# Layer 3's attention: scores computed once and kept in SBUF, instead of once by rows and once by columns

## The chip, the cores and the metric

The kernel runs on one core of a Trainium2 chip. Four compute engines work side by side, each through its own queue in order: TensorE (PE; its weight loads are PEld), VectorE (DVE), ScalarE (ACT) and GpSimd (POOL). SyncE (SP) issues transfers. TensorE writes only to PSUM, eight banks of 2 KB on each of 128 partitions; VectorE and ScalarE read it, GpSimd works in SBUF alone. The metric is the device time of one execution, in microseconds. All numbers are fp32.

## The reference, cut to what matters

Four layers follow one another on four batches of 512 rows of 512 channels: a cross attention (layer 0), two recurrent layers of the RWKV kind (1 and 2), and layer 3, a cross attention of perceiver form with an MLP. Only layer 3 is touched. Its inputs are the context (`x` below), the result of layer 2 (`latents`), and a key mask of the context:

```
h = concatenate([x, latents], axis=1)              # 1024 keys
q = (latents @ q_w + q_b)                          # 512 queries, 16 heads of 32
k, v = h @ kv_w + kv_b
attn = einsum('bkhd,bnhd->bhkn', q, k) / 32
attn = where(mask, attn, -inf)                     # 512 context keys may be masked
attn = softmax(attn)
out = einsum('bhkn,bnhd->bkhd', attn, v) @ out_w + out_b + latents
out = rmsnorm(out) * postnorm_w
return gelu(out @ mlp_w1 + mlp_b1) @ mlp_w2 + mlp_b2 + latents
```

The softmax needs the largest score of every query, over all 1024 keys, ahead of the exponentials.

## The kernel before

Layers 0 to 2 end at about 2402 us, layer 3 fills the rest. The engines' instructions stand in the order in which the program writes them; `layer3` is a generator whose first parts are run beside the tail of the recurrent layers (each `yield` ahead of `"closed"` gives the word back to `recurrent`), and the loop at the end of `layer3` writes the rest.

A unit is one batch and four heads (the four 32-row strips `r` of a 128-channel block `m`), so there are 16 units. In the loop, each unit has eight steps (`NB` = 8 blocks of 128 keys), and three units are in work at once:

- `least(u, lt, a)` (L1196) makes, for one block of 128 queries and one half of the keys, four scores of 128 queries by 512 keys (`psc`), queries on partitions. VectorE adds the key mask as a row (`nm`, or `zeros`) and takes the minimum of the negated scores into one column of `mx`, written by L1206.
- `spread` (L1217), once a unit, turns that column by TensorE transposes (`pb`) into rows that are alike on all partitions, and ScalarE copies them to `mb`.
- `turned(u, s)` (L1230), a unit later, makes the scores again, keys on partitions (`pst`: 128 keys by 512 queries for four heads); VectorE subtracts `mb` on the way out of PSUM (L1237).
- `weights` (L1239): ScalarE's exponential over 2048 elements, with the mask as a bias per partition for the context keys; GpSimd adds the blocks into `acc`, whose sum over partitions is the softmax's denominator.
- `values` (L1262), two steps later: the products with `v` add up in one PSUM bank, `po`.
- `counted`, `inverted`, `divided`: the denominator by a product of `acc` with ones, its reciprocal, and the product with `po` into `y`.

Between these stand two further generators that the loop takes piece by piece: `prep` (q, k and v of the next unit: five pieces, and two more for a new batch in `begin`), and `finish` (output product, residual, norm, transposes and the MLP of the batch before: 38 pieces of one to eight products). `piece(early)` or `piece(rest)` takes one per step, and `behind` decides whether a second one is taken. `finish` of the last batch comes after the loop. Matrix products of a whole array go through the helper `mm` (L73), so its line holds most of TensorE's work; there the tiles tell the groups apart: `ph` and `po<-l_m,hT` are the MLP, `pout` the output product, `pq`, `pk`, `pv` belong to `prep`. ScalarE changes its table of functions whenever an exponential follows a gelu or the other way round.

PSUM in the loop is one pool of seven banks for everything (`ps_s`) and one bank for `po`.

Of the kernel before, what the change touches and what calls it, by code (L numbers as in the profile page):

```python
# [8 lines left out]
F32 = mybir.dt.float32  # L9
# [21 lines left out]
def tile_xattn_rwkv_perceiver(ctx: ExitStack, tc: tile.TileContext, t: dict, out: bass.AP):  # L31
# [1070 lines left out]
    def layer3():  # L1102
# [3 lines left out]
        T2 = 2 * P  # L1106
        with ExitStack() as pools:
# [10 lines left out]
            nc.vector.tensor_scalar(cols[:, :, 0], cols[:, :, 0], -1.0 / HD, None, ALU.mult)  # L1118
# [3 lines left out]
            zeros = cp.tile([P, L], F32, name="zeros")  # L1122
            nc.gpsimd.memset(zeros, 0.0)
# [3 lines left out]
            b2 = row_bcast(cp, t["L3_b2"], C, "b2")  # L1127
            st = [{} for _ in range(B)]

            def begin(b):  # L1130
# [4 lines left out]
                mi = bp.tile([P, L], I32, tag="sc", name="mi", bufs=2)  # L1135
                nc.sync.dma_start(mi, t["mask3"][b : b + 1, :].to_broadcast([P, L]))
                nm = bp.tile([P, L], F32, tag="nm", name="nm", bufs=2)
                nc.vector.tensor_scalar(nm, mi, 0.0, 1e30, ALU.is_equal, ALU.mult)
                d["nm"] = nm, zeros
# [5 lines left out]
                for k in range(KC):  # L1145
                    pt = ps_s.tile([P, L], F32, tag="s", name="ptx")
                    for i in range(LT):
                        nc.tensor.transpose(pt[:, i * P : (i + 1) * P], xn[b][i][:, k * P : (k + 1) * P], ident)
                    nc.scalar.copy(xT[:, k, :], pt)
                    if k % 2:  # L1150
                        yield

            def prep(b, m):
# [7 lines left out]
                q = d["q", m] = bp.tile([P, L], F32, tag="q", name="q", bufs=3)  # L1161
                pm = ps_s.tile([P, L], F32, tag="s", name="pq")
                mm(pm, [(w3["q"][:, k, :], d["xT"][:, k, :]) for k in range(KC)])
                nc.scalar.activation(q, pm, AF.Identity, bias=cols[:, m, 0:1], scale=-1.0 / HD)
                yield
                kT = d["k", m] = bp.tile([P, 2, L], F32, tag="kT", name="kT", bufs=3)
                v = d["v", m] = bp.tile([P, NB, P], F32, tag="v", name="v", bufs=3)
                for a, src in enumerate((d["cT"], d["xT"])):
# [3 lines left out]
                    yield  # L1172
                    pm = ps_s.tile([P, LT, P], F32, tag="s", name="pv")
# [9 lines left out]

            def row_scores(lhsT, rhs, name):

                ps = []
                for r in range(NR):
                    rs = slice(32 * r, 32 * r + 32)  # L1190
                    psc = ps_s.tile([P, L], F32, tag="s", name=name)
                    nc.tensor.matmul(psc, lhsT[rs], rhs[rs], start=True, stop=True, tile_position=(32 * r, 0))  # L1192
                    ps.append(psc)
                return ps

            def least(u, lt, a):  # L1196

                b, m = u
                d = st[b]
                if (lt, a) == (0, 0):  # L1200
                    d["mx", m] = bp.tile([P, 2, LT, NR], F32, tag="mx", name="mx", bufs=2)
                mx = d["mx", m]
                ps = row_scores(d["q", m][:, lt * P : (lt + 1) * P], d["k", m][:, a, :], "psc")
                for r in range(NR):
                    sc = bp.tile([P, L], F32, tag="sc", name="sc", bufs=2)
                    nc.vector.tensor_tensor_reduce(  # L1206
                        sc,
                        ps[r],
                        d["nm"][a],
                        1.0,  # L1210
                        mx[:, 0, lt, r : r + 1] if a else 3.0e38,
                        ALU.add,
                        ALU.min,
                        mx[:, a, lt, r : r + 1],
                    )

            def spread(u):  # L1217

                b, m = u
                d = st[b]  # L1220
                mb = d["mb"] = bp.tile([P, NR, L], F32, tag="mb", name="mb", bufs=1)
                for r in range(NR):
                    pb = ps_s.tile([P, L], F32, tag="s", name="pb")
                    for lt in range(LT):
                        nc.tensor.transpose(  # L1225
                            pb[:, lt * P : (lt + 1) * P], d["mx", m][:, 1, lt, r : r + 1].to_broadcast([P, P]), ident
                        )
                    nc.scalar.copy(mb[:, r, :], pb)

            def turned(u, s):  # L1230

                b, m = u
                d = st[b]
                ps = row_scores(d["k", m][:, s // LT, s % LT * P : (s % LT + 1) * P], d["q", m], "pst")
                w = d["w", s] = sp.tile([P, NR, L], F32, tag="aT", name="aT", bufs=3)
                for r in range(NR):
                    nc.vector.tensor_tensor(w[:, r, :], ps[r], d["mb"][:, r, :], ALU.subtract)  # L1237

            def weights(u, s):  # L1239

                b, m = u
                d = st[b]
                w = d["w", s]
                wf = w.rearrange("p r l -> p (r l)")
                if s < LT:
                    nc.scalar.activation(wf, wf, AF.Exp, bias=d["mc"][:, s : s + 1], scale=-1.0)  # L1246
                else:
                    nc.scalar.activation(wf, wf, AF.Exp, scale=-1.0)  # L1248
                if s == 1:
                    acc = d["acc", m] = sp.tile([P, NR, L], F32, tag="acc", name="acc", bufs=1)  # L1250
                    nc.gpsimd.tensor_tensor(acc, d["w", 0], w, ALU.add)  # L1251
                elif s > 1:
                    nc.gpsimd.tensor_tensor(d["acc", m], d["acc", m], w, ALU.add)  # L1253

            def columns(po, lhsT, rhs, **kw):

                for r in range(NR):
                    nc.tensor.matmul(  # L1258
                        po[32 * r : 32 * r + 32, :], lhsT(r), rhs[:, r, :], tile_position=(0, 32 * r), **kw
                    )  # L1260

            def values(u, s):  # L1262

                b, m = u
                d = st[b]
                if s == 0:
                    d["po"] = ps_o.tile([P, L], F32, tag="o", name="po")
                v = d["v", m]
                columns(
                    d["po"], lambda r: v[:, s, 32 * r : 32 * r + 32], d["w", s], start=(s == 0), stop=(s == NB - 1)  # L1270
                )

            def counted(u):

                b, m = u
                d = st[b]
                pn = d["pn"] = ps_s.tile([P, L], F32, tag="s", name="pn")
                columns(pn, lambda r: ones, d["acc", m], start=True, stop=True)

            def inverted(u):  # L1280
                d = st[u[0]]
                rs = d["rs"] = bp.tile([P, L], F32, tag="sc", name="rs", bufs=2)
                nc.vector.reciprocal(rs, d["pn"])

            def divided(u):
                b, m = u
                d = st[b]
                if "y" not in d:
# [220 lines left out]
```

## Time and profile before

| | us |
|---|---|
| median of 3 runs | 3721.07 (3719.92 to 3722.31) |
| span of the profiled execution, first to last instruction | 3715.9 |
| layer 3 from the first score after the recurrent layers (2402.6) | 1313 |
| of it attention of the first batch, to the first `pout` (2642.0) | 239 |
| of it attention beside the finishing of batches 0 to 2 (to 3576.4) | 934 |
| of it the last finish | 140 |

The profiled execution is a run of its own, whose time is its span and what lies around it: 5.2 us less by its span than the median of the runs. The page gives busy time over the whole span; in a group's line stand line, engine, operation, tile out<-in, shapes and count, then busy time and the mean of one in ns, then the idle time ahead of it and what ended it. A window's line gives, for each engine, busy time and the number of instructions, then the granted TensorE clock as a share, DMA share and GB/s. A timeline's line is start, length, engine, line, operation, and in brackets the idle time before it.

### The profile page before, as it was taken

To read this page: it belongs to the slowest core of one execution; us is meant where nothing else is said; L and a number is where in the kernel's file an instruction comes from. 1 tells how busy PE (TensorE), PEld (TensorE's weight loads), DVE (VectorE), ACT (ScalarE), POOL (GpSimd) and SP (SyncE) were. 2 spreads that over 40 slices of the span, in tenths; PEclk is the share of its full clock that TensorE was granted. 3 is DMA by queue.
4 is the path that set the end of the run, shared out by engine and by line. 5 is a ranking of instruction groups with operands and counts; after the bars stand their busy time and mean duration, and the time that the engine had idled before them with its cause. 6 is when DMAs were issued, how large, how long until landed. Compare 5 with 4: busy or idle time off the path is not lost. (4 is left out here: it accounts for less than half of the span.)

```text
span 3715.9 us, 52436 instructions
## 1 busy us (share of the span) xinstructions
PE 3545.8 (95%) x20544; PEld 1885.9 (51%) x20544; DVE 2728.7 (73%) x4601; ACT 1675.7 (45%) x2550; POOL 1743.4 (47%) x850
## 2 busy tenths in 40 slices
PE   8999999998899999999999988999999999999989
PEld 3333333365566665666666644444455444544446
DVE  6777777679988888888888883388855676667531
ACT  4777676544444444444444433233344334434421
POOL 4777777524444444444444443065533343444430
PEclk9999999999999999999999998999999999999999
DMA  4000000056677777777777775300022212121223
GB/s 154 24 12 24 12 9 21 24 130 140 146 177 175 177 187 182 176 175 177 177 175 177 177 167 134 102 26 18 23 88 77 72 52 88 60 71 35 97 97 125
DMA packets 188806, 386.67 MB, mean 104 GB/s; under 512 B 18128, under 2 KB 44880, under 8 KB 186512
## 3 DMA queue, kind: packets, MB, share of 16 engines
q1 hardware_dynamic: 150256, 251.72, 21.2%
q0 software_dynamic: 38304, 131.61, 19.4%
q8 instruction: 162, 2.65, 0.3%
q14 instruction: 84, 0.69, 0.1%
HBM read 247.50 MB, written 4.19 MB: 68 GB/s over the span
## 5 line engine op out<-in xcount | busy, mean ns | idle before, releaser
L1253 POOL TENSOR_TENSOR acc<-acc,aT 128x2048 f32<-128x2048 f32 x96 | 436.2, 4544 | 336.2 <-ACT aT L1248 219.6
L292 POOL TENSOR_TENSOR aT<-aT,nmT 128x1536 f32<-128x1536 f32 x124 | 428.6, 3460 | 206.1 <-ACT aT L290 182.8
L254 DVE CUSTOM_DVE_ANT_0 sc<-psc,nm 128x512 f32<-128x512 f32 x512 | 353.8, 691 | 146.8 <-PE psc L242 89.1
L1237 DVE TENSOR_TENSOR aT<-pst,mb 128x512 f32<-128x512 f32 x512 | 317.5, 681 | 163.2 <-PE pst L1192 163.2
L871 DVE TENSOR_TENSOR ry<-kv,o_r 128x1024 f32<-128x1024 f32 x256 | 398.6, 1598 | 7.2 <-PE pm L73 0.5
L866 DVE TENSOR_TENSOR_SCAN kv<-W,kv 128x1032 f32<-128x1032 f32 x128 | 295.9, 2311 | 0.0
L584 POOL DMA_DIRECT2D kv<-A x127 | 111.4, 877 | 358.0 <-DVE kv L839 220.0
L290 ACT COPY aT<-pst 128x512 f32<-128x512 f32 x372 | 196.5, 594 | 177.2 <-PE pst L279 176.8
L298 ACT ACTIVATE aT<-aT 128x2048 f32<-128x2048 f32 x128 | 246.7, 1929 | 5.5 <-POOL aT L292 4.8
L73 PE MATMUL ph<-nT,l_m 128*128 128x256 f32 x1024 | 235.9, 385 | 0.0
L73 PE MATMUL po<-l_m,hT 128*128 128x512 f32 x512 | 233.1, 601 | 0.0
L73 PEld LDWEIGHTS ph<-nT,l_m 128*128 128x128 f32 x1024 | 191.8, 191 | 64.2 <-issue 24.8
L1206 DVE CUSTOM_DVE_ANT_0 sc<-psc,zeros,mx 128x512 f32<-128x512 f32 x256 | 176.6, 745 | 56.2 <-PE psc L1192 47.1
L279 PE MATMUL pst<-q,km 32*128 32x512 f32 x1024 | 206.3, 639 | 9.4 <-DVE mxs L254 5.8
L1248 ACT ACTIVATE aT<-aT 128x2048 f32<-128x2048 f32 x64 | 122.3, 1910 | 190.6 <-DVE aT L1237 185.7
L1246 ACT ACTIVATE aT<-aT,mc 128x2048 f32<-128x2048 f32 x64 | 128.1, 2002 | 162.6 <-DVE aT L1237 156.3
L1206 DVE CUSTOM_DVE_ANT_0 sc<-psc,nm 128x512 f32<-128x512 f32 x256 | 161.1, 684 | 52.2 <-PE psc L1192 52.2
L242 PE MATMUL psc<-km,q 32*128 32x512 f32 x1024 | 197.8, 650 | 0.8 <-ACT q L223 0.8
L885 PE MATMUL py<-ry,k 128*32 128x512 f32 x1024 | 161.9, 625 | 38.3 <-DVE ry L871 25.6
L1192 PE MATMUL pst<-q,kT 32*128 32x512 f32 x1024 | 183.1, 649 | 0.0
L1192 PE MATMUL psc<-kT,q 32*128 32x512 f32 x1024 | 171.0, 644 | 12.3 <-DVE aT L1237 11.5
L1251 POOL TENSOR_TENSOR acc<-aT 128x2048 f32<-128x2048 f32 x16 | 72.5, 4532 | 234.2 <-ACT aT L1246 234.2
(266 smaller groups left out, 6999.6 us busy)
## 6 DMA issues: line engine op xcount, KB each, us to landing
l_m<-in_L_W SPq DMA_DIRECT2D x64, 1024.0 KB, 5.1
kv<-A POOLq DMA_DIRECT2D x127, 516.0 KB, 6.1
L_wk<-in_L_Wk SPq DMA_DIRECT2D x16, 1024.0 KB, 8.0
L_wr<-in_L_Wr SPq DMA_DIRECT2D x16, 1024.0 KB, 7.2
L_wv<-in_L_Wv SPq DMA_DIRECT2D x16, 1024.0 KB, 5.8
L_wg<-in_L_Wg SPq DMA_DIRECT2D x16, 1024.0 KB, 7.6
L_wo<-in_L_Wo SPq DMA_DIRECT2D x64, 256.0 KB, 4.9
L_fk<-in_L_fWk SPq DMA_DIRECT2D x16, 1024.0 KB, 6.8
```

The source lines that it names most:

```text
L73: nc.tensor.matmul(ps, lhsT, rhs, start=(i == 0), stop=(i == len(pairs) - 1))
L242: nc.tensor.matmul(psc, d["q"][g][rs, lt * P : (lt + 1) * P], d["km"][rs, a, :], start=True, stop=True, tile_position=(32 * r, 0),)
L254: nc.vector.tensor_tensor_reduce(sc, ps[r], d["nm"][lt], 1.0, -3.0e38, ALU.add, ALU.max, mxs[:, a, lt, c : c + 1])
L279: nc.tensor.matmul(pst, d["km"][rs, a, s * P : (s + 1) * P], d["q2", a][rs, :], start=True, stop=True, tile_position=(32 * r, 0),)
L292: nc.gpsimd.tensor_tensor(w[:, n:, :], w[:, n:, :], nmT[:, None, :].to_broadcast([P, NR - n, L]), ALU.add)
L298: nc.scalar.activation(w, w, AF.Exp)
L866: nc.vector.tensor_tensor_scan(flat(kv), flat(W[g % 2]), flat(kv), 0.0, ALU.mult, ALU.add)
L871: nc.vector.tensor_tensor(y, kv[:, 4 * h : 4 * h + 4, None, :TP].to_broadcast([P, 4, 2, TP]), d["r"][:, i].rearrange("p (o m) -> p o m", o ...
L1192: nc.tensor.matmul(psc, lhsT[rs], rhs[rs], start=True, stop=True, tile_position=(32 * r, 0))
L1206: nc.vector.tensor_tensor_reduce(sc, ps[r], d["nm"][a], 1.0, mx[:, 0, lt, r : r + 1] if a else 3.0e38, ALU.add, ALU.min, mx[:, a, lt, r : ...
L1237: nc.vector.tensor_tensor(w[:, r, :], ps[r], d["mb"][:, r, :], ALU.subtract)
L1253: nc.gpsimd.tensor_tensor(d["acc", m], d["acc", m], w, ALU.add)
```

## The change

Each unit is split in two halves of 256 queries (`h`), so there are 32 half units; each has four steps (`NS` = 4), a step being two blocks of 128 keys (`e`) for four heads and 256 queries. Scores are made once, keys on partitions, in a PSUM tile `ps` of four banks, of which there is one buffer (`ps_w`). VectorE takes the maximum of that tile into a running maximum `run` in SBUF (`largest`; masked keys get their bias in the same operation), and ScalarE copies the tile, with the mask as its bias, into SBUF (`kept`; six buffers `w`). After four steps `gathered` turns `run` by eight transposes (`ptm`) and VectorE reduces them to the maximum of each query, `spread` turns it back as before. In the next four steps `lowered` subtracts it in place, SBUF from SBUF, the exponential follows, then `values` and the GpSimd additions (`added`). A one-element `tick` is set by VectorE in each step and copied by GpSimd ahead of its additions, so that these begin behind VectorE's maximum of that step. The loop takes `prep` in steps 0, 4 and 6 of a unit (two, two and three pieces) and `finish` in the other five (two each); `prep` of the second unit runs beside the recurrent tail, where unit 0's `least` ran. PSUM is four banks for `ps`, three for all else, and one for `po`.

Beside this: `out_b` is added to the residual by GpSimd in `begin` and taken off `b2`, the scaling by 1/rms goes from VectorE to ScalarE (`scaled`), the transposes for the MLP's second half come after its first half, and the mask's row form with its transfers is gone.

```diff
-                mi = bp.tile([P, L], I32, tag="sc", name="mi", bufs=2)
-                nc.sync.dma_start(mi, t["mask3"][b : b + 1, :].to_broadcast([P, L]))
...
+                for x in xn[b]:
+                    nc.gpsimd.tensor_tensor(x, x, ob, ALU.add)
...
+            def scores(i):
+                (b, m, h), j = place(i)
+                d = st[b]
+                ps = ps_w.tile([P, NR, 2, HQ], F32, tag="w", name="ps")
+                a, s = divmod(2 * j, LT)
+                for e in range(2):
+                    for r in range(NR):
+                        rs = slice(32 * r, 32 * r + 32)
+                        nc.tensor.matmul(
+                            ps[:, r, e, :],
+                            d["k", m][rs, a, (s + e) * P : (s + e + 1) * P],
+                            d["q", m][rs, h * HQ : (h + 1) * HQ],
...
+            def kept(i):
...
+                w = ws[i] = sp.tile([P, NR, 2, HQ], F32, tag="w", name="w", bufs=6)
+                if a:
+                    nc.scalar.copy(w.rearrange("p r e q -> p (r e q)"), ps.rearrange("p r e q -> p (r e q)"))
+                else:
+                    for e in range(2):
+                        nc.scalar.activation(
+                            w[:, :, e, :], ps[:, :, e, :], AF.Identity, bias=d["mc"][:, s + e : s + e + 1]
+                        )
+            def largest(i):
...
+                for e in range(2):
+                    mc = d["mc"][:, s + e : s + e + 1]
+                    if a:
+                        nc.vector.tensor_tensor(run, ps[:, :, e, :], run, ALU.max)
+                    elif j or e:
+                        nc.vector.scalar_tensor_tensor(run, ps[:, :, e, :], mc, run, ALU.add, ALU.max)
+                    else:
+                        nc.vector.tensor_scalar(run, ps[:, :, e, :], mc, None, ALU.add)
+            def gathered(u):
...
+                for c in range(2):
+                    pt = ps_s.tile([P, NR, P], F32, tag="s", name="ptm")
+                    for r in range(NR):
+                        nc.tensor.transpose(pt[:, r, :], d["run"][:, r, c * P : (c + 1) * P], ident)
+                    nc.vector.tensor_reduce(mx[:, c, :], pt, AX.X, ALU.max)
+            def lowered(i):
...
+                nc.vector.tensor_tensor(w, w, mb, ALU.subtract)
+            def weights(i):
+                w = ws[i].rearrange("p r e q -> p (r e q)")
+                nc.scalar.activation(w, w, AF.Exp)
+            def added(i):
...
+                if j == 0:
...
+                    nc.gpsimd.tensor_tensor(d["acc", m, h], w[:, :, 0, :], w[:, :, 1, :], ALU.add)
+                else:
+                    for e in range(2):
+                        nc.gpsimd.tensor_tensor(d["acc", m, h], d["acc", m, h], w[:, :, e, :], ALU.add)
...
+            LOW, VAL, CNT = NS, NS + 1, NS + 3
+            yield from chain(begin(0), prep(0, 0), prep(0, 1))
+            first.close()
+            yield "closed"
+            sp = opened("l3s", 2)
+            ps_s = opened("l3ps", 3, space=PSUM)
+            ps_w = opened("l3pw", 1, space=PSUM)
+            po = opened("l3po", 1, space=PSUM).tile([P, 2, HQ], F32, name="po")
...
+            for i in range(NU + CNT + 1):
...
+                if i >= NS and i % NS == 0 and i <= NU:
+                    gathered(units[i // NS - 1])
+                if 0 <= i - VAL < NU:
+                    values(i - VAL)
...
+                    counted(units[done // NS])
+                if i < NU:
+                    scores(i)
+                if i >= NS and i % NS == 0 and i <= NU:
+                    spread(units[i // NS - 1])
+                low = i - LOW
+                if 0 <= low < NU and low % NS:
+                    lowered(low)
+                    weights(low)
+                if i < NU:
+                    largest(i)
+                    kept(i)
+                if 0 <= low < NU and low % NS == 0:
+                    lowered(low)
+                    weights(low)
+                if 0 <= low < NU:
+                    tick = sp.tile([P, 1], F32, tag="tick", name="tick")
+                    nc.vector.memset(tick, 0.0)
+                    nc.gpsimd.tensor_copy(mark, tick)
+                if 0 <= i - VAL < NU:
+                    added(i - VAL)
...
+                if c in (0, 4, 6):
+                    taken(early, 3 if c == 6 else 2)
+                else:
+                    taken(rest, 2)
```

## Prediction

> **What bounds the kernel now.** I read the page first, for the share of each engine:
>
> ```profile
> PE 3545.8 (95%) x20544; PEld 1885.9 (51%) x20544; DVE 2728.7 (73%) x4601; ACT 1675.7 (45%) x2550; POOL 1743.4 (47%) x850
> ```
>
> That is a mean over four layers. The change touches layer 3 alone, so I took the windows by stage: the first batch's attention, three stretches in which attention runs beside the finishing of the batch before (first `pout` at 2642.0), and the last finish.
>
> ```profile
> core 0: us, PE busy (x) PEld busy (x) DVE busy (x) ACT busy (x) POOL busy (x), PEclk, DMA share, GB/s
> 2402.00:2622.00 220.00, 218.42 (x1224) 99.44 (x1225) 181.14 (x409) 80.58 (x64) 123.75 (x29) 1.00 0.09 27
> 2622.00:2941.00 319.00, 315.84 (x1620) 154.96 (x1619) 210.99 (x440) 125.66 (x124) 135.03 (x37) 0.99 0.20 66
> 3272.00:3576.00 304.00, 296.02 (x1462) 144.00 (x1460) 186.39 (x367) 120.37 (x120) 137.48 (x37) 0.98 0.22 74
> 3576.00:3716.00 140.00, 129.35 (x436) 82.48 (x432) 28.82 (x42) 17.61 (x41) 7.11 (x8) 0.96 0.31 105
> ```
>
> TensorE is busy through all of layer 3; VectorE reaches 82% in the first stretch, 61 to 66% later. The TensorE timeline shows how a block is made: whole matrix products fill the time between the scores.
>
> ```profile
> 2916.98 3.72 PE L73 MATMUL ph<-nT,l_m 128*128 128x256 f32 x16
> 2920.63 1.14 PE L1192 MATMUL pst<-q,kT 32*128 32x512 f32 x8
> 2921.70 1.06 PE L1258 MATMUL po<-aT,v 128*32 128x512 f32 x8
> 2922.70 1.14 PE L1192 MATMUL psc<-kT,q 32*128 32x512 f32 x8
> 2923.77 3.70 PE L73 MATMUL po<-l_m,hT 128*128 128x512 f32 x8
> ```
>
> Start to start, a group of four score matmuls costs 1.07, a group of values 1.0, a piece of finish or prep 3.63 to 3.77 us. The groups give the prices of the other engines:
>
> ```profile
> L1253 POOL TENSOR_TENSOR acc<-acc,aT 128x2048 f32<-128x2048 f32 x96 | 436.2, 4544 | 336.2 <-ACT aT L1248 219.6 <-ACT aT L1246 116.6
> L1248 ACT ACTIVATE aT<-aT 128x2048 f32<-128x2048 f32 x64 | 122.3, 1910 | 190.6 <-DVE aT L1237 185.7 <-POOL acc L1253 4.7
> L1228 ACT COPY mb<-pb 128x512 f32<-128x512 f32 x64 | 32.7, 604 | 0.6 <-PE pb L1225 0.6
> L833 DVE TENSOR_TENSOR kv<-vr,o_k 128x1024 f32<-128x1024 f32 x128 | 155.5, 1215 | 25.2 <-ACT S L857 25.1
> L946 DVE TENSOR_TENSOR y<-y,bc 128x1024 f32<-128x1024 f32 x16 | 19.6, 1224 | 18.9 <-ACT bc L944 18.9
> ```
>
> Last, two timelines that decide the new step. VectorE's sum of two SBUF operands (normally 0.69) takes 1.63 because GpSimd's add, from 2671.30 to 2676.02, is in the way; and after 3.16 us of idle TensorE's next groups run at half pace (six score instructions in 3.27, where eight take 1.14).
>
> ```profile
> 2671.30 4.72 POOL L1253 TENSOR_TENSOR acc<-acc,aT 128x2048 f32<-128x2048 f32 x1
> ...
> 2674.94 1.63 DVE L1304 TENSOR_TENSOR ao<-ao,x 128x512 f32<-128x512 f32 x1
> ...
> 2680.36 3.27 PE L1192 MATMUL psc<-kT,q 32*128 32x512 f32 x6 [3.16 <-DVE aT L1237]
> ```
>
> **The new step.** There are 32 half units (four heads, 256 queries) of four steps, 128 steps in all. On TensorE a step is 1.1 of scores (two groups of 256 columns; twice the 0.44 that L689's 256-column groups take, plus the 0.2 by which 1.07 exceeds two such) and 1.0 of values. `psc`, 8.6 us a unit, goes. Each half unit adds eight transposes for the maximum, 0.95 by `pb`'s 1.84 for sixteen; the eight `pb` stay, and `pn` is 0.55. So a unit asks TensorE for 16.8 + 3.8 + 1.1 = 21.7 instead of 28.1 us (psc 8.6, pst 8.6, po 8.0, pn 1.0, pb 1.84): 6.4 less.
>
> VectorE, per step: subtract 2048 elements, 2.29 (1.224 for 1024 and 0.691 for 512 give the slope); maximum, two of 1024 from PSUM, 2.4. Per half unit: two reductions 1.4, reciprocal 1.7 (half of L1283's 3.35), product 0.4, the four ticks 0.4. ScalarE, per step: the exponential 1.91 and the new copy out of PSUM, 2.2 with the mask (0.687 for 512 plus 0.427, twice), 1.9 without. GpSimd: adds of 1024 cost 2.35 (between 1.27 for 512 and 4.53 for 2048), seven a half unit.
>
> **The new waits.** The score tile takes four banks and has one buffer. In the built program the copy waits for VectorE's maximum, and the next scores wait for the copy. So where nothing else is to be done a step costs scores 1.1, maximum 2.4, copy 2.2 and three hand-overs of some 0.07: 5.9 us. The subtraction has both operands in SBUF, and so do GpSimd's adds: 4.7 + 2.29 = 7.0 if each excludes the other. The row above shows VectorE held; the reverse shows in the same add: L1253 takes 4.72 where its median is 4.53, each time that a 1.5 us VectorE operation at L1309 ends inside it. I take 7.0; the other end is 5.9. At a half unit's border the chain is longer: from the end of the last maximum, transposes 1.0, values 1.0, scores 1.1, maximum 2.4, subtraction 2.3 to 3.4 (behind an add), exponential 1.9, then that block's values 1.0, the next scores 1.1, their maximum 2.4: about 15.5 for two steps, with hand-overs. Two more steps at some 5.6 to 7.0, one of them with the division, bring a half unit without pieces to 28.5. TensorE idles over 3 us twice in it and then runs at half pace; by the 3.27 us row that costs some 2 us. 30.5 a half unit, 61 a unit; ends 25.5 (VectorE's own 23.3 and one border gap of 2.2) and 34 (each border and every third step at half pace).
>
> The Trainium skill, SBUF — State Buffer, section Who interferes with whom, speaks against this subtraction: a VectorE instruction with two SBUF inputs contends with a GpSimd instruction that reads SBUF, and the one issued second is blocked until the first ends. By that rule the step without pieces is 7.0 and the first batch as summed below; were the lock one-sided it would be 5.9, and the first batch some 30 us shorter. The trace agrees for the side that it shows (1.63 instead of 0.69).
>
> **The sum by stages**, against the profiled execution: span 3715.9, median of the runs 3721.1, so 5.2 lie around it.
>
> 1. Up to the last recurrent product, 2402.6 now. Unit 0's eight `psc` groups leave that tail: 9.9 us on the chain of waits. Four new adds of `ob` (1.27 each) stand on GpSimd before `gn_rs` (L935), which the chain passes: +5. 2397.6.
> 2. To the first finish: step 38. Steps 0 to 3 have no subtraction, 5.9 each, and a first half unit of 27 with no GpSimd backlog: 48. Then 30 steps at 61 per eight: 229. Sum 277, against 2402.6 to 2642.0, 239: **+38**. prep's five pieces a unit lie in the border gaps.
> 3. Steps 38 to 134, beside finishes 0 to 2, two pieces of 3.65 a step: TensorE 9.4, VectorE under 8.2, ScalarE 8.6 (with two table loads of 1.28 and two to four gelus of 0.47), GpSimd 4.7. TensorE's content: scores 90 x 1.1, values 95 x 1.0, 23 borders x 1.9, 25 `pn` x 0.55 (together 252), ten preps x 18.8 and a piece (192), two begins x 4, three finishes x 135 (ph 235.9, po 233.1, pout 59.5, ptn 12.3, by four): 857. Gaps: step 6 of a unit has one piece, 0.5 x 12; two steps without a piece, 5.5 each; unit 15 has no prep to do, 25; the end of the last half unit 16; nT before its first product 9; gelus inside a pair of pieces 9: 76. 933, against 2642.0 to 3576.4, 934: **-1**. The 77 us that `psc` saves in twelve units go into these gaps and into the finishing pieces that now find less time to hide in. Ends of the gaps: 20 (most are covered) and 120.
> 4. Last finish: 139.5 now; the second half's transposes no longer stand ahead of the first product (4.1 us of idle) but the division comes before it, 2.5: 138.5.
>
> 2397.6 + 277 + 933 + 138.5 = 3746; plus 5.2: **3751 us**, 0.8% slower.
>
> Moved at no cost: scaling by 1/rms goes from VectorE (23.7 us in all) to ScalarE, hidden while a step has pieces; `ob`'s add leaves VectorE (11 us) for GpSimd, which has 20 of each 50 us busy. The row mask and its DMAs go; they lay beside other work. Table loads stay at 73.
>
> **Rivals.** (a) The gaps of stage 3 close: steps with two pieces leave VectorE and ScalarE time to be ahead, and TensorE's 95% busy row speaks for it. With 20 instead of 76 the time is 3695; it decides, against the loss of stage 2, from gaps under 38 us on: faster. (b) No measurable difference: stage 2 at its one-sided 5.9 a step, 30 less: 3721. (c) ScalarE becomes the bound in stage 3: its 8.6 stand only 0.8 under TensorE's 9.4, and the copy sits in its queue behind an exponential that waits for VectorE, with all gelus behind it. At 10.5 a step, 97 steps give 1018: 3836. Against it: 120 to 130 us busy in 304 to 331 now. That the work is not removed is excluded: the built order has no `psc` any more.
>
> **Numbers.** Forecast (3729 to 3800) 0.56, (a) 0.26, (b) 0.10, (c) and worse 0.08. Faster 0.26, same 0.10, slower 0.64; 0.2%, 7.4 us, is about what a measurement of this kernel can tell from no change. The range: stage 2 by 25.5 to 34 a half unit is -40 to +26, stage 3 by 20 to 120 is -56 to +44, stage 1 ±5. All together would be 3650 to 3826; 8 in 10 is 3695 to 3800. Within the forecast alone 3729 to 3790.
>
> **What would show it.** Right: in the first batch TensorE under 75% busy, a lower granted clock there, some 60 us between every second `pb`; subtractions far above 2.3 us on average; in the middle some 75 to 79 us a unit with TensorE still above 90%. Wrong: subtractions at 2.3 and units of 52 in the first batch (one-sided or no lock); middle units of 71 (rival a); ScalarE above 90% with TensorE waiting for the copy in the middle (rival c). The number falls first with the gaps of stage 3, which no row of before shows.

## The result and the profile after

The changed kernel takes 3804.1 us (median of 4 runs, 3798.5 to 3805.7), the kernel before 3720.6 on the same chip: ratio 1.0221, 95% interval 1.0206 to 1.0235. That is 83 us slower where 30 were forecast, and 4 us beyond the upper end of the range. The span of the profiled execution is 3802.2.

The windows of the changed kernel, cut at its first score (2398.1), at the first `pout` of each of the four finishes, and at its end; columns as before:

```profile
core 0: us, PE busy (x) PEld busy (x) DVE busy (x) ACT busy (x) POOL busy (x), PEclk, DMA share, GB/s
2398.00:2731.00 333.00, 220.01 (x1778) 130.59 (x1778) 217.22 (x193) 163.18 (x128) 192.70 (x99) 0.76 0.06 18
2731.00:3054.00 323.00, 297.85 (x2011) 184.55 (x2013) 207.18 (x202) 191.12 (x180) 171.85 (x101) 0.96 0.22 72
3054.00:3376.00 322.00, 296.65 (x2024) 183.99 (x2020) 208.19 (x202) 191.14 (x180) 172.67 (x101) 0.97 0.22 73
3376.00:3669.00 293.00, 252.79 (x1645) 153.29 (x1638) 175.48 (x173) 165.09 (x154) 161.17 (x91) 0.94 0.20 66
3669.00:3802.00 133.00, 127.80 (x432) 81.03 (x430) 19.54 (x34) 20.13 (x45) 7.13 (x8) 0.99 0.34 115
```

| stage | before | forecast | after |
|---|---|---|---|
| first score at | 2402.6 | 2397.6 | 2398.1 |
| first batch, to the first `pout` | 239 | 277 | 332.6 |
| beside finishes 0 to 2 | 934 | 933 | 938.0 |
| last finish | 139.5 | 138.5 | 133.6 |

By the span, the profiled execution lies 56 us above the forecast's 3746, and all of that is in the first batch (55.6; the other stages nearly cancel). There TensorE is 66% busy, at a granted clock of 0.76. No engine is full: VectorE has 65%, GpSimd 58%, ScalarE 49%. So it is waits, and the lower clock, that set this stage. TensorE's list of waits, first for this stage, then for the middle (us in all, times, longest):

```profile
PE ps L1199 <- ACT w L1220: 32.5, 8, 10.9
PE ptm L1249 <- DVE tick L1450: 22.3, 8, 3.4
PE po L1293 <- DVE y L1323: 22.3, 7, 4.8
PE po L1293 <- ACT w L1276: 19.4, 8, 5.5
PE ps L1199 <- ACT w L1217: 7.5, 3, 4.6
...
PE po L1293 <- ACT w L1276: 28.9, 18, 7.2
PE po L73 <- ACT hT L1374: 18.8, 12, 2.9
PE ph L73 <- DVE nT L1357: 16.3, 3, 5.5
PE po L1293 <- DVE y L1323: 13.8, 9, 5.1
PE ptx L1145 <- ACT xT L1146: 9.9, 2, 4.9
```

Scores waiting for the copy and transposes waiting for the maximum were in the forecast; values waiting for the division (`y`) were not. (The two halves of a unit have their sums in the one bank of `po`; in `bank`, below, where each has a bank of its own, this wait is gone.) The timeline of TensorE over most of a half unit shows what the waits do to the pace:

```profile
2507.38 1.15 PE L1199 MATMUL ps<-q,kT 32*128 32x256 f32 x16
2512.48 1.93 PE L1293 MATMUL po<-w,v 128*32 128x256 f32 x16 [3.95 <-ACT w L1276]
2514.19 1.08 PE L1293 MATMUL pn<-acc,ones 128*32 128x256 f32 x8
2515.29 1.21 PE L1199 MATMUL ps<-q,kT 32*128 32x256 f32 x16
2516.43 3.84 PE L73 MATMUL pv<-w3v,xT 128*128 128x128 f32 x32
2521.34 1.07 PE L1293 MATMUL po<-w,v 128*32 128x256 f32 x16 [1.07 <-DVE y L1323]
2522.34 1.15 PE L1199 MATMUL ps<-q,kT 32*128 32x256 f32 x16
2526.44 1.97 PE L1249 MATMUL ptm<-ident,run 128*128 128x128 f32 x8 [2.95 <-DVE tick L1450]
2528.34 1.94 PE L1293 MATMUL po<-w,v 128*32 128x256 f32 x16
```

After a gap of 3 to 4 us a group of values takes 1.93 instead of 1.07, eight transposes 1.97 instead of 1.04; after 1.07 us of gap the pace is kept. And this is the start of the stage, which has no subtraction yet:

```profile
2398.07 1.14 PE L1199 MATMUL ps<-q,kT 32*128 32x256 f32 x16
2398.25 0.69 DVE L1035 SCALAR_TENSOR_TENSOR xr<-xr,pv 128x512 f32<-128x512 f32 x1 [2.76 <-PE pv L73]
2399.23 0.86 POOL L584 DMA_DIRECT2D x<-xr  x1 [2.59 <-DVE xr L1035]
2405.18 1.28 DVE L1240 TENSOR_SCALAR run<-ps,mc 128x1024 f32<-128x1024 f32 x1 [6.25 <-DMA x<-xr]
2406.50 1.28 DVE L1238 SCALAR_TENSOR_TENSOR run<-ps,mc,run 128x1024 f32<-128x1024 f32 x1
2407.95 2.12 ACT L1220 ACTIVATE w<-ps,mc 128x1024 f32<-128x1024 f32 x2 [16.04 <-DVE run L1238]
2410.12 2.09 PE L1199 MATMUL ps<-q,kT 32*128 32x256 f32 x16 [10.90 <-ACT w L1220]
```

The maximum of the first tile waits 6.25 us for the transfer that carries the last rows out of the recurrent layers (`x<-xr`). The likely reason is in the program: the pool of `run` is opened when the recurrent layers' pools have been closed, so it can lie on memory that this transfer still reads. No run tested that. TensorE idles for 10.9 us, and the next scores run at half pace (2.09).

Taken apart by steps, the 55.6 us between the forecast's 277 and 332.6 are three:

- The start: scores of step 8 stand at 2463.7, 65.6 after the first; 48 was forecast. +17.6.
- Steps 8 to 38: 257.9 (scores of step 38 at 2721.6); 229 was forecast. +28.9.
- The end of the stage was counted one step early: step 38 takes pieces of `prep`, and the first `pout` (2730.6) is taken in step 39. +9.0.

### The profile page after: what moved, and what is told of

It reads as the page before. It is cut to its first block, busy times and chain, and to the rows that moved or that the text cites. A ratio compares the mean times of both kernels' runs of the same rounds, so it can differ in the third digit from the quotient of the medians.

```text
span 3802.2 us, 54498 instructions
## 1 busy us (share of the span) xinstructions
PE 3443.3 (91%) x21952; PEld 1972.7 (52%) x21952; DVE 2711.7 (71%) x3637; ACT 1930.9 (51%) x2758; POOL 1915.7 (50%) x1106
## 5 line engine op out<-in xcount | busy, mean ns | idle before, releaser
L1288 POOL TENSOR_TENSOR acc<-acc,w 128x1024 f32<-128x1024 f32 x192 | 491.5, 2560 | 7.8 <-POOL mark L1451 0.2
L254 DVE CUSTOM_DVE_ANT_0 sc<-psc,nm 128x512 f32<-128x512 f32 x512 | 354.1, 692 | 148.0 <-PE psc L242 90.3
L1451 POOL COPY mark<-tick 128x1 f32<-128x1 f32 x128 | 92.7, 724 | 556.9 <-DVE tick L1450 378.1
L1276 ACT ACTIVATE w<-w 128x2048 f32<-128x2048 f32 x128 | 244.5, 1911 | 200.4 <-DVE w L1272 187.7
L1272 DVE TENSOR_TENSOR w<-w,mb 128x2048 f32<-128x2048 f32 x128 | 321.5, 2522 | 1.8 <-ACT mb L1265 1.8
L298 ACT ACTIVATE aT<-aT 128x2048 f32<-128x2048 f32 x128 | 246.8, 1929 | 5.6 <-POOL aT L292 4.9
L1293 PE MATMUL po<-w,v 128*32 128x256 f32 x2048 | 160.1, 437 | 84.4 <-ACT w L1276 48.3
L1236 DVE TENSOR_TENSOR run<-ps,run 128x1024 f32<-128x1024 f32 x128 | 156.5, 1223 | 77.4 <-PE ps L1199 75.2
L1199 PE MATMUL ps<-q,kT 32*128 32x256 f32 x2048 | 170.1, 453 | 40.2 <-ACT w L1220 32.5
L1220 ACT ACTIVATE w<-ps,mc 128x1024 f32<-128x1024 f32 x128 | 135.6, 1110 | 118.0 <-DVE tick L1450 62.0
```

Of the source, the lines that this page charges most:

```text
L254: nc.vector.tensor_tensor_reduce(sc, ps[r], d["nm"][lt], 1.0, -3.0e38, ALU.add, ALU.max, mxs[:, a, lt, c : c + 1])
L298: nc.scalar.activation(w, w, AF.Exp)
L1199: nc.tensor.matmul(ps[:, r, e, :], d["k", m][rs, a, (s + e) * P : (s + e + 1) * P], d["q", m][rs, h * HQ : (h + 1) * HQ], start=True, stop ...
L1236: nc.vector.tensor_tensor(run, ps[:, :, e, :], run, ALU.max)
L1272: nc.vector.tensor_tensor(w, w, mb, ALU.subtract)
L1276: nc.scalar.activation(w, w, AF.Exp)
```

## Experiments

Theory A (chain): scores, maximum, copy, next scores, through the one PSUM tile, set a step. Theory B (exclusion): GpSimd's additions and VectorE's subtraction shut each other out, and that sets a step, as the prediction took it. Theory C (pace): TensorE's half pace after gaps lies on the path. Theory D: values wait for the division. Differences below are against the changed kernel's 3804.1; the kernel before took 3720.6 to 3723.5 beside these runs, so a difference of some 3 us between two runs says little. Stages are those of the profiled executions. In the cuts of the edits, `...` stands for lines left out.

**The additions taken away** (`no_adds`).

```diff
-                if j == 0:
+                if j == NS - 1:
                     d["acc", m, h] = sp.tile(...)
                     nc.gpsimd.tensor_tensor(d["acc", m, h], w[:, :, 0, :], w[:, :, 1, :], ALU.add)
-                else:
-                    for e in range(2):
-                        nc.gpsimd.tensor_tensor(d["acc", m, h], d["acc", m, h], w[:, :, e, :], ALU.add)
```

> Left out: GpSimd's additions of the denominator, all but the one of the last step of a half unit (one instruction of 2.36 us in place of seven), so the denominator is the sum of a quarter of the terms. Theory B (exclusion: a step of the first batch lasts 7 us or more because GpSimd's adds, 4.7, and VectorE's subtraction, 2.29, both with their operands in SBUF, shut each other out): subtractions come down from 2.52 to 2.3 us on average, the first stage (first score group to first pout, 332.6 us now) loses 1.1 us in each of some 34 steps, 35 to 45 us, total some 3762. Theory A (chain: scores, maximum, copy, scores through the one PSUM score tile set the step, and the subtraction fits into VectorE's wait for the next scores even when it is held): first stage -10 at most, total 3792 or more. Theory C (TensorE's half pace) says nothing of it: no change of the clock, 0.76.

Measured: 3785.9, -18.2; the first stage 326.1 (-6.5), the middle 925.6 (-12.4). The group of subtractions, first of the changed kernel, then of this one (busy us, mean ns):

```profile
L1272 DVE TENSOR_TENSOR w<-w,mb 128x2048 f32<-128x2048 f32 x128 | 321.5, 2522 | 1.8 <-ACT mb L1265 1.8
```

```profile
L1272 DVE TENSOR_TENSOR w<-w,mb 128x2048 f32<-128x2048 f32 x128 | 291.1, 2285 | 1.8 <-ACT mb L1265 1.8
```

GpSimd is held in its turn: in the changed kernel its one-element copy, 0.18 us by itself, takes 2.17 when a subtraction has begun just before it, and ends with it:

```profile
2512.93 2.29 DVE L1272 TENSOR_TENSOR w<-w,mb 128x2048 f32<-128x2048 f32 x1
2513.09 2.17 POOL L1451 COPY mark<-tick 128x1 f32<-128x1 f32 x1 [4.75 <-DVE tick L1450]
```

The lock is real and goes as B says (2.52 to 2.285 us), but the first stage moves as A says. Over the 28 steps 8 to 36 it is worth 4.3 us, 0.15 a step, where the prediction had put 1.1. The total lies between the two expectations, because most of the gain is in the middle, where neither looked for it.

**Two score tiles with a change-over** (`split`), and the same without the additions.

```diff
-                ps = ps_w.tile([P, NR, 2, HQ], F32, tag="w", name="ps")
+                ps = [ps_w.tile([P, 2, 2, HQ], F32, tag="w", name="ps") for _ in range(2)]
...
-            ps_w = opened("l3pw", 1, space=PSUM)
+            ps_w = opened("l3pw", 2, space=PSUM)
...
-                    largest(i)
-                    kept(i)
+                    most(0)      # maximum of strips 0, 1
+                    copied(1)    # copy of strips 2, 3
+                    most(1)
+                    copied(0)
```

> The score tile is two tiles of two banks; VectorE takes the maximum of strips 0 and 1 while ScalarE copies strips 2 and 3, then they change over. Per step VectorE has 0.3 us more (four instructions of 512 for two of 1024), ScalarE 0.3 to 0.5 more. Theory A: the chain of a step falls from 1.1 + 2.5 + 2.0 + 0.2 = 5.8 to 1.1 + 1.4 + 1.4 + 0.2 = 4.1, VectorE's own work (5.05 a step) is then the bound, so the first stage loses 1.5 us a step or more, 45 to 60 us, total 3740 to 3760. Theory B: the step stays at 7 us (adds 4.7 and subtraction 2.29, one after the other), first stage -15 at most, total 3785 or more. In the middle, where whole products fill TensorE's time, both expect under 20 us of change.

> Both of the last two edits; left out is the same part of the denominator. Theory A alone: as with the two tiles alone, within 10 us. Theory B alone: as without the adds alone, within 10 us. If the two bind one behind the other (the chain at 5.8 under the exclusion at 7.0): more than the sum of the two alone, a first stage of VectorE's 5.05 a step and the borders, 26 to 27 us a half unit instead of 34.4, so 60 to 75 us less, total 3730 to 3740.

Measured: 3886.5, **+82.4**, and without the additions 3834.7, +30.6. Both theories missed it, and none of the three outcomes expected of the second run came. The timeline of `split` says why:

```profile
2510.18 2.71 DVE L1274 TENSOR_TENSOR w<-w,mb 128x2048 f32<-128x2048 f32 x1
...
2512.81 1.53 DVE L1235 SCALAR_TENSOR_TENSOR run<-ps,mc,run 128x512 f32<-128x512 f32 x2
2512.92 1.91 ACT L1278 ACTIVATE w<-w 128x2048 f32<-128x2048 f32 x1 [2.26 <-DVE w L1274]
...
2515.14 2.42 ACT L1224 ACTIVATE w<-ps,mc 128x512 f32<-128x512 f32 x4 [0.31 <-POOL acc L1290]
2516.44 1.54 DVE L1235 SCALAR_TENSOR_TENSOR run<-ps,mc,run 128x512 f32<-128x512 f32 x2 [2.11 <-ACT w L1224]
...
2517.91 2.29 DVE L1274 TENSOR_TENSOR w<-w,mb 128x2048 f32<-128x2048 f32 x1
```

The copy of strips 2 and 3 stands in ScalarE's queue behind an exponential, which waits for the subtraction; the second maximum now waits for that copy, and the next subtraction stands behind the maximum. So the edit closed a loop through both queues: subtraction, exponential, copy, maximum, subtraction. Taking the additions away gives 51.8 us here, against 18.2 without the loop: the subtractions again get 0.23 us shorter (2.557 to 2.329), and the copy no longer waits for additions to give a buffer `w` back; the two were not separated.

**Two score tiles in order** (`split2`): as above, with `most(0)`, `most(1)`, `copied(0)`, `copied(1)`.

> The two score tiles of the run with the change-over, without the change-over: VectorE takes the maximum of strips 0 and 1, then of 2 and 3; ScalarE copies in the same order, each copy behind its maximum alone. If that run was 82 us slower because VectorE's second maximum stood behind ScalarE's copy, and that behind an exponential: total back to 3804 or under; by theory A the first copy starts 1.2 us earlier, VectorE has 0.3 more a step, so -0.9 in 34 steps, total 3770 to 3780. If it was slower because of the doubled instructions (0.3 on VectorE and 0.3 to 0.5 on ScalarE in 128 steps, 75 to 100 us): total 3870 or more.

Measured: 3786.8, -17.3; first stage 323.5 (-9.1), middle 931.4 (-6.6). So the change-over, not the doubled instructions, cost the 82. But A's gain of 0.9 a step is not there: steps 8 to 36 take 237.5 instead of 239.9; most of what is gained in the first stage comes ahead of them. Step 1 of a unit falls from 6.4 to 4.5 us, and step 2 rises from 8.2 to 8.9: what one step gains, others give back.

**The maximum from the copy** (`sbufmax`).

```diff
-                    largest(i)      # reads ps in PSUM
-                    kept(i)
+                    kept(i)
+                    largest(i)      # reads w in SBUF, mask already in it
...
```

> ScalarE copies first, and VectorE takes the maximum from the copy in SBUF, so the next scores wait for the copy alone. Theory A: the loop scores, copy, scores is 1.1 + 2.1 + 0.2 = 3.4 a step instead of 5.8, VectorE's own 4.8 is the bound where GpSimd leaves it alone: first stage 27 to 29 a half unit at half pace or better, -35 or more, total 3770 or less. Theory B: the maximum now has two operands in SBUF as the subtraction has, so maximum 2.5, subtraction 2.3 and adds 4.7 shut each other out, 9.4 a step: 38 a half unit or more in the first stage, +30 there; in the middle 9.4 a step is just TensorE's own 9.4, +0 to +40; total 3835 to 3875, maximum and adds both above their prices on average.

Measured: 4021.7, +217.6, half units of 43 to 44 us at the beginning. This is slower than either theory said. Its timeline shows the loop of `split` once more, with whole tiles:

```profile
2496.63 2.73 DVE L1268 TENSOR_TENSOR w<-w,mb 128x2048 f32<-128x2048 f32 x1
...
2499.39 1.91 ACT L1272 ACTIVATE w<-w 128x2048 f32<-128x2048 f32 x1 [7.33 <-DVE w L1268]
2501.60 1.87 ACT L1217 COPY w<-ps 128x2048 f32<-128x2048 f32 x1 [0.30 <-POOL acc L1284]
2503.50 2.48 DVE L1234 TENSOR_TENSOR run<-w,run 128x1024 f32<-128x1024 f32 x2 [4.14 <-ACT w L1217]
```

2.73, 1.91, 1.87 and 2.48 with their hand-overs are 9.3 us from one subtraction to the end of the maximum that the next one stands behind. What the lock adds to the maximum itself is little (1.26 us on average in this stage, 1.223 from PSUM without a mask), so this run does not separate A from B; it shows that here the order within the two queues cost more than either.

**TensorE kept busy** (`warm`).

```diff
...
+                if not got and i < 38:      # no piece taken in this step
+                    pd = ps_s.tile([P, L], F32, tag="s", name="pd")
+                    for _ in range(3):
+                        nc.tensor.matmul(pd, ident, vb, start=True, stop=True)
```

> Three products of 128x512 whose result nobody reads (0.907 us each at full pace) stand on TensorE at the end of each of the first 38 steps that has no piece of its own. Theory C (half pace: after gaps of 3 to 5 us the groups of a border take 1.9 to 2.1 instead of 1.0 to 1.1, some three groups a half unit, on the path): granted clock of the first stage from 0.76 to 0.95 or more, first stage -2 to -3 us a half unit, 18 to 28 in all, total 3776 to 3786. If the half pace lies beside the other engines' work: clock up, time within 6 us. If the idle gaps do not set the clock: clock at 0.8 or less, and the products at half pace (5.4 us a step) make the first stage longer by 20 or more.

Measured: 3775.6, **-28.5**; first stage 305.0, middle 936.8. The window of this stage:

```profile
2400.00:2705.00 305.00, 258.76 (x1939) 143.29 (x1936) 216.26 (x193) 163.28 (x128) 192.88 (x99) 0.96 0.07 19
```

The clock goes from 0.76 to 0.96, VectorE, ScalarE and GpSimd do the same work as before, and the stage is 27.6 us shorter though TensorE does more. This is C at the upper end of what it expected: half pace cost 3.0 us in each of the seven half units of steps 8 to 36 (218.8 instead of 239.9 in all), and 5.5 in the first eight steps.

**Values and division apart** (`bank`), and **no division** (`nodiv`).

```diff
...
-            ps_s = opened("l3ps", 3, space=PSUM)
+            ps_s = opened("l3ps", 2, space=PSUM)
...
-            po = opened("l3po", 1, space=PSUM).tile([P, 2, HQ], F32, name="po")
+            po = opened("l3po", 2, space=PSUM)
+            po = [po.tile([P, HQ], F32, tag="o", name="po") for _ in range(2)]
```

```diff
-                nc.vector.reciprocal(rs, d["pn"])
+                nc.vector.tensor_copy(rs, d["pn"])
```

> Each half unit's sums of values lie in a PSUM bank of their own (two for po), and the pool of the other products has two banks instead of three. Theory D (values wait for the division because both halves share a bank: 22.3 us of TensorE's idle time before po <-DVE y in the first stage, 13.8 in the middle): these waits go, first stage -10 to -20, middle -5 to -14, total 3770 to 3790. Rival: the third bank was worth as much (transposes, products and pieces then wait for the reader of the one before): 3804 or more. If the wait only moves to the next thing (scores wait for the copy anyway): 3800 to 3806.

> Left out: the reciprocal (a copy of pn stands in its place, so the values are multiplied by the denominator). 1.75 us of VectorE become some 0.4, 32 times. If the division lies on the path of each half unit of the first stage: -1.3 in each of nine, -12, and up to as much in the middle; total 3780 to 3792. If it lies beside other work: 3800 to 3806.

Measured: `bank` 3827.1, +23.0: the wait for `y` is gone from its list, and the first stage is 5.6 us shorter, but with two banks for the other products the middle grows by 27.7. `nodiv` 3790.7, -13.4: first stage -8.0, middle -2.9 in the profiled execution. The division is on the path, at about 1 us a half unit of the first batch.

**All together.** `warm` with `split2`, and then with both parts left out as well.

> The unread products that keep TensorE at full pace in the first 38 steps, and the two score tiles taken in order. Alone they gave -28.5 and -17.3 us. If half pace and the one score tile cost in different places: -46, total 3758. If both shorten the same gaps: -30 or less, total 3774 or more.

> Left out: the same part of the denominator as in the run without adds, and the reciprocal. The four edits together: products that keep the pace, two score tiles in order, no adds, no division. Alone they gave -28.5, -17.3, -18.2 and -13.4. If each cost lies in a place of its own: -77, total 3727, a half unit of the first stage 27 to 28 us. If loops of nearly the same length stand behind one another, so that taking one away shows the next: clearly more than the sum, total 3705 or less, a half unit at VectorE's own 24 to 26. If one loop that none of the four touches is the bound: less than the sum, total 3745 or more, a half unit over 29.

Measured: 3761.4 (-42.7, nearly the sum of 45.8) and 3712.9 (-91.2, more than the sum of 77). The second lies between what was expected if the costs add up and if they hide one another, and the stages tell why. In steps 8 to 36 they add up: `warm`, `split2`, `no_adds` and `nodiv` alone save 21.1, 2.4, 4.3 and 8.5 us, 36.3 together, and `warm_all` saves 36.7. What goes beyond the sum is in the middle, 38.8 (938.0 to 899.2) where the four alone save 23.1. Mean time from scores to scores in us, over the steps 8 to 31, by the place of the step in its unit (0 and 4 are borders; one of the three values behind step 6 holds three pieces of `prep`):

| step | 0 | 1 | 2 | 3 | 4 | 5 | 6 | 7 | unit |
|---|---|---|---|---|---|---|---|---|---|
| changed kernel | 11.1 | 6.4 | 8.2 | 8.3 | 10.8 | 7.3 | 9.3 | 7.8 | 69 |
| `warm` | 10.4 | 6.3 | 7.0 | 6.9 | 10.1 | 7.3 | 8.9 | 6.3 | 63 |
| `warm_all` | 10.6 | 5.8 | 5.9 | 5.8 | 10.1 | 5.4 | 8.9 | 6.5 | 59 |

A unit was forecast at 61, its half pace included. Borders hardly move: with the clock up, scores 1.07, `pb` 0.93, two pieces of `prep` 7.0 and values 1.0 fill 10.0 us of TensorE without a gap. So in steps 8 to 36 no cost hid another. With all four out a half unit of them still takes 29.0, where the prediction had 28.5 with the additions, the division and the one score tile still in it.

**One more product in each step of the middle** (`pad`).

```diff
                 else:
                     taken(rest, 2)
+                if 40 <= i < 134:
+                    pd = ps_s.tile([P, L], F32, tag="s", name="pd")
+                    nc.tensor.matmul(pd, ident, vb, start=True, stop=True)
```

> The changed kernel with one more product of 128x512 that nobody reads, 0.907 us, at the end of each of steps 40 to 133 (94 of them, 85 us of TensorE). Theory of the prediction's third stage (TensorE's own work sets a step that has two pieces, and only some steps have gaps): two thirds or more show, +55 to +85, total 3860 to 3890. Rival (the middle is set by the waits for ScalarE and VectorE as the first stage is, TensorE's 91 us of idle time there take up the products): +30 or less, total under 3835.

Measured: 3851.5, +47.4; the middle 990.3, +52.3. Of 85 us of added TensorE work 61% shows: between the two expectations, less than the prediction's picture had it.

**Only the edits of `finish`, in the kernel before** (`finish_only`), and its two parts.

```diff
+            nc.gpsimd.tensor_tensor(b2, b2, ob, ALU.subtract)
...
+                for x in xn[b]:
+                    nc.gpsimd.tensor_tensor(x, x, ob, ALU.add)
...
-                    nc.vector.tensor_tensor(ao, pm, ob, ALU.add)
-                    nc.vector.tensor_tensor(ao, ao, x, ALU.add)
+                    nc.vector.tensor_tensor(ao, pm, x, ALU.add)
...
-                    nc.vector.tensor_scalar(ao, ao, rstd, None, ALU.mult)
...
+                        scaled(*aos[lt - 1])          # on ScalarE, one piece later
...
-                    nTs.append(nT)                    # the order of the transposes
-                    yield
-                for h in range(L // T2):
-                    nT = nTs[h]
+                    yield
```

`order_only` has the last hunk alone, `relief_only` all but the last.

> The kernel before with one part of the change alone: ob goes into x and b2 on GpSimd, the scaling by 1/rms on ScalarE one piece later, and the second half's transposes behind the first half's products; the attention is as before. By the prediction's terms: the last recurrent product 5 us later (four adds of 1.27 ahead of gn_rs), the middle unchanged, the last finish 1 us shorter: +4, total 3727. Rival: the last finish is 6 us shorter, as in the changed kernel (133.6 instead of 139.5), and VectorE's 35 us less shorten the waits in the middle: total 3712 to 3721.

> The kernel before, with one edit: the second half's transposes and nT stand behind the first half's products, instead of all four pairs of transposes in a row. In the kernel before a finish then shows 3.16 us of idle TensorE at psc (waiting for VectorE, which has nT's four evictions in its queue) and the next groups at half pace (3.25, 1.97); in the run with all the finish's edits this is gone. If the order gives the gain: three finishes x 7 us in the middle and 4 to 6.5 in the last, -22 to -27 of the run's -24, total 3694 to 3699. If VectorE's relief gives it: within 6 us of the kernel before.

> The kernel before, with the other edits of finish: ob inside x and b2 by GpSimd, the scaling by 1/rms on ScalarE one piece later; transposes in the order of before. VectorE has 35 us less to do in four finishes, none of it in the stretch of the four pairs of transposes: total 3715 to 3726 if the order is what counts (adds ahead of gn_rs +2 to +5); 3700 or less if the relief is.

Measured: `finish_only` 3696.9, ratio to the kernel before 0.9935 (0.9918 to 0.9952); `relief_only` 3702.6, 0.9948 (0.9934 to 0.9963); `order_only` 3724.9, 1.0011 (1.0002 to 1.0021). So **the small edits alone make the kernel before faster by 24 us**, below both expectations, and VectorE's relief alone gives 19 of them (the intervals of the two runs overlap); the order of the transposes, which the expectation held for the cause, gives nothing by itself. In the kernel before, VectorE's queue at a finish looks like this:

```profile
2678.24 1.48 DVE L1309 TENSOR_SCALAR ao<-ao,rms 128x512 f32<-128x512 f32 x1 [0.66 <-POOL rms L79]
2679.63 2.47 DVE L1237 TENSOR_TENSOR aT<-pst,mb 128x512 f32<-128x512 f32 x4
```

The scaling waits for GpSimd's root and takes 1.48 us, ahead of the subtractions that free the score banks; the scores then start at 2680.36 after 3.16 us without work and run at half pace. Such waits for `aT` are 10.5 us in the middle of the kernel before. In `relief_only` they are gone. These are TensorE's waits in the middle and the window of it, first before, then in `relief_only`:

```profile
PE psc L1192 <- DVE aT L1237: 10.5, 3, 4.2
PE pn L1258 <- POOL acc L1253: 3.8, 1, 3.8
2642.00:3576.00 934.00, 919.71 (x4625) 452.65 (x4624) 595.55 (x1225) 368.97 (x366) 398.84 (x108) 0.99 0.22 72
```

```profile
PE pn L1261 <- POOL acc L1256: 3.8, 1, 3.8
2649.00:3565.00 916.00, 911.95 (x4624) 449.50 (x4623) 567.99 (x1199) 376.46 (x378) 407.20 (x116) 1.00 0.22 73
```

Of the 18 us that this stage loses, 10 are idle time of TensorE, and 8 are its own: the same products take 912.0 instead of 919.7, which fits fewer of them at half pace (granted clock 1.00 instead of 0.99).

By stages `finish_only` has 241 for the first batch, 913.5 for the middle (-21) and 133.0 for the last finish (-6.5). Whether the sum with `ob` or the scaling counts more was not separated.

## Why the prediction was wrong, point by point

- **First score at 2397.6**: 2398.1, and that it is so near is partly luck. `finish_only`, which has the adds of `ob` and keeps `psc`, starts at 2404.5, 1.9 later than the kernel before and not 5; then `psc` was worth 6.5 there and not 9.9. Runs with the changed kernel's tail start between 2395.9 and 2402.2, so neither term is measured well.
- **Prices**: right where it counts. Scores 1.15, values 1.07, transposes 1.04 to 1.09, `pn` 0.55 to 0.61 at full pace; subtraction 2.285 undisturbed; maximum 2.45 to 2.6, a little dearer with a mask (1.283 for 1024, 1.223 without); copy 2.12 and 1.86.
- **Stage 2, the term that failed**: "48" for the start and "229" for the rest, 277 against 332.6. Four parts of it, worked out from the runs.
  1. The start, +17.6. The two terms of "48", four steps at 5.9 and a half unit of 27, add up to 50.6, so 2.6 is a slip in the sum. Steps 0 to 3 took 32.7 instead of 23.6: the 6.25 us wait for the recurrent layers' last transfer was not foreseen at all, and steps 1 to 4 run at half pace, which the sum had given to later steps only. The first half unit took 33.0 instead of 27.
  2. Half pace: 3.0 us a half unit (`warm`) instead of 2, +7.1 in the seven half units from step 8 to 36.
  3. What is left of a half unit with the pace kept: 31.3 instead of 28.5, +19.3 in the same seven. In `warm`, some 6 of this stand in step 30 alone, which took 12.9 us where steps 14 and 22 took 7.0: this unit has the two pieces of the next batch's `begin` beside its five of `prep`, and step 30 takes three. The prediction let pieces lie in gaps at no cost and had no `begin` in this stage. Some 10 stand in the two steps at each border, 16.9 on average instead of 15.5, and 3 in the other steps. The division was in the sum and is on this path (`nodiv`: 33.1 a half unit instead of 34.3); why the border steps are longer was not taken apart further.
  4. The stage's end: one step early, +9.0, and 2.5 in steps 36 to 38.

  Together 55.5. The range allowed this stage no more than +26, because it varied only the length of a half unit.
- **"I take 7.0"** (the exclusion a step): wrong as a cause. The Trainium skill, SBUF — State Buffer, section Who interferes with whom, says that issue order decides who blocks. The trace agrees in both directions: the subtraction takes 2.52 on average instead of 2.285, and the copy behind the tick 2.17 instead of 0.18 while a subtraction runs. But the block cost little of the stage: `no_adds` gave 0.15 a step, and step 1 of a unit, with a subtraction in it, took 6.4 on average. That a blocked instruction costs time only where its engine is late fits this, and was not tested by itself. Rival (b), in which stage 2 loses 30 us for a lock on one side, falls with it: without any lock it loses 6.5.
- **Stage 3, 933**: 938, with 847 of TensorE's work (857 forecast) and 91 of gaps (76 forecast). That the size holds is partly luck, since 10 less of work and 15 more of gaps nearly cancel, and the comparison behind it did not hold: it was read as no change against 934. The edits of `finish`, "moved at no cost" and put at nothing beyond the last finish, alone take 21 us out of this stage; so against `finish_only` the new attention costs 24.5 us there. `psc`'s 77 us went into gaps, as forecast: idle TensorE rises from 14 to 91.
- **Stage 4, 138.5**: 133.6. A gain of 1 was forecast, from the order of the transposes less a division (139.5 - 4.1 + 2.5 is 137.9, another small slip). 6 were gained, and `relief_only` has them (132.6) without that order, while `order_only` has none (140.9).
- **Rivals (a) and (c)**: the gaps did not close. ScalarE is 58% busy in the middle, so it is no bound there; but the 28.9 us of values waiting for its exponential are the longest wait.
- **A sum that does not come out**: VectorE's own "23.3" a half unit, an end of the range; the terms listed for it add up to 22.7.

Against `finish_only`, then, the account of the change is: the attention costs +91 in the first batch and +24.5 in the middle and saves 6.5 in the tail ahead of it, which is about the scatter of the first score; the edits of `finish` save 24.

## What to carry to other kernels

Work that is saved on the busiest engine is worth something only in stages where that engine sets the time; in a stage of waits, write down every loop through the queues, in the order in which each engine's instructions stand, before choosing the one that binds. An edit meant to shorten one loop can close another through two in-order queues, and here that cost more than it saved. And try the side edits of a large change by themselves: here they were the gain, and the version to keep is `finish_only`, at 3696.9 us.

## What the runs showed of the hardware that was not expected

Products whose result nobody reads made a stage 27.6 us shorter, by keeping the granted clock at 0.96 instead of 0.76; gaps of 3 to 4 us were enough to lose it, a gap of 1.1 us was not. The same additions on GpSimd cost 51.8 us in one order of two queues (`split`) and 18.2 in another, though they lengthened each subtraction by 0.23 to 0.24 us in both.
